# An adaLN block with attention and experts: the setup written out in a fixed order, partly inside the first iterations, with two staging buffers, and the slots blanked from the load queue

## The chip, the cores and the metric

The kernel runs on one core of a Trainium2 chip. The metric is the time of one execution on the device in microseconds. TensorE (PE; its weight loads are PEld) does the matmuls, VectorE is DVE, ScalarE is ACT, GpSimd is POOL, and SyncE (SP) issues most of the DMAs. Every engine works through its own instructions in order; a DMA is issued by an engine's queue and then runs on the core's 16 DMA engines.

## The reference

The input x has 4096 tokens (2 batches of 2048) of width 256. A modulation of six vectors per batch is computed from c, and its two gates are kept away from zero. Then come windowed attention (16 heads of 64, window 128) and a layer of 8 experts, two of which a token uses. The feed-forward layer is cut here to its shape:

```python
mod = (_silu(c) @ wmod).reshape(2, 6, 1, -1)
sa, ca, ga, sb, cb, gb = mod[:, 0], ..., mod[:, 5]
ga = (2 * (ga >= 0) - 1) * jnp.maximum(jnp.abs(ga), 0.25)   # gb likewise
h = layernorm(x) * (1 + ca) + sa
x = x + ga * (window_attention(h @ Wqkv) @ Wout)            # causal, 128 keys
h = layernorm(x) * (1 + cb) + sb
# gate: softmax of h @ gate_w.T + gate_b, top 2; at most 640 slots per expert and choice
# expert: relu(xb @ W1 + b1) @ W2 + b2, weighted by the gate's probability
x = x + gb * experts(h)
```

## The kernel before, in words

**Numbers in two halves.** A product of two fp32 matrices is made of three fp32r matmuls: each operand has an upper half (`hi`, a rounding copy made on ScalarE) and a lower half (`lo`, the rest, a subtraction made on DVE or POOL). `split` makes both from a raw tile, `passes` issues the three matmuls (L232), and `part` (L298) does the split for what comes out of PSUM. A raw piece of weights is 128x1024 fp32, 512 KB.

**Stages.** Up to about 30 us comes the setup (L322 to L463 and the projection at L1159): loading, the modulation, the norm of the first 256 tokens (`norm(0)`, a generator that does one step for each `next`), and the splitting of Wqkv (six pieces) and Wout (two pieces). The raw pieces go into four buffers (two of the pool `stage`, two of the pool `sp`). The order in this part is chosen by a planner that knows costs and dependences. Three small loads, the gate's weights and bias `gw` and `gbias` and the experts' `b1r`, are issued by ScalarE. All the modulation is done here: 16 small matmuls into `mod_cols` (the shift and scale of the first norm, as columns `cols`) and eight into `mod_rows` (the other four vectors), which go through a tile `wide4` and the DRAM tile `rowd` and come back spread over partitions as `rows` and `gbr`.

**Attention.** From the scores of iteration 0 at 29.90 us to about 720 us the kernel is in 64 iterations and three more to drain. A group g is 256 tokens, and each group takes four iterations of two head pairs (four heads). Iteration w runs a software pipeline: it projects q and k for the heads of iteration w+1 (L279), one quarter of v, makes the scores of its own heads (L502), packs the two diagonal blocks with the masks (`pack`, L519 to L527), takes the maximum and starts the exponentials (`exps`, L550); it normalizes the heads of iteration w-1 (L560 on POOL), turns those of w-2 (`turn`, `unpack`, L583) and multiplies them with v (`values`, L607), and applies Wout to those of w-3 (`out_project`). In this part the order is the program's order on all five engines (`manual_schedule`). Work that comes once for each group (the norm of the next group, and `close`, which ends a group: residual, second norm, gate, scatter of the rows to expert slots) is a generator whose steps are put at named places of an iteration by `place(work, w, [...])`. The place "1H" is the point H of iteration w+1; the points come in the order A, B, M, H, C, then the scores, S, V. PSUM tiles for all this come from `bank`, a ring of six.

**Slots.** `xbuf` in DRAM has 10,240 slots of 274 words, which `clear` must blank before the rows of tokens are scattered into them from iteration 12 on (L820). In each of iterations 1 to 4 ScalarE's queue issues four blanking DMAs (L468) of 685 KB from one tile `blank`:

```python
for i in range(2 * w - 2, 2 * w):
    if 0 <= i < E:
        clear(i)          # two DMAs of 640 slots each
```

**Experts.** From about 720 us the slots of each expert are taken in items of up to six tiles of 128; an item has eight steps f, each with a first layer (relu with L939, L940, L941) and, two steps later, a second layer. While the first item of an expert runs, the weights of the next are brought in four pieces at f = 0, 2, 4, 6, each a load (L136) and a split (L127). After the third item the planner orders the instructions again, save those kept in program order, such as these splits.

Of the kernel before, what the change touches and what calls it, by code (L numbers as in the profile page):

```python
# [17 lines left out]
P = 128  # L18
# [10 lines left out]
def adaln_block_kernel(  # L29
# [94 lines left out]
    def split(hi, lo, raw, scale=None, eng=nc.vector, keep=False):  # L124

        if scale is None:
            parts = [nc.scalar.copy(hi, raw), eng.tensor_tensor(lo, raw, hi, ALU.subtract)]  # L127
            for p in parts if keep else ():
                tc.keep_in_program_order(p)
        else:  # L130
            nc.scalar.mul(hi, raw, scale)
            nc.vector.scalar_tensor_tensor(lo, raw, scale, hi, ALU.mult, ALU.subtract)

    def load(src, shape, name, pool=stage):
        raw = pool.tile(shape, FP, tag="raw", name=f"raw_{name}", bufs=2)
        nc.sync.dma_start(out=raw, in_=src)  # L136
        return raw

    def load_split(hi, lo, src, shape, name, scale=None, pool=stage, eng=nc.vector):
        split(hi, lo, load(src, shape, name, pool), scale, eng)  # L140

    class Expert:
# [24 lines left out]
        def use(self, i):  # L167
            wa, wb = self.parts()
            if i < 2:
                s = slice(i * FF // 2, (i + 1) * FF // 2)  # L170
                hi, lo = wa[:, 0, :, s], wa[:, 1, :, s]
            else:
                s = slice((i - 2) * NF // 2, (i - 1) * NF // 2)
                hi, lo = wb[:, 0, s, :], wb[:, 1, s, :]
            split(hi, lo, self.raws.pop(i), keep=self.e > 1)

        def steps(self):

            ahead = 2 if self.e < 2 else 0
            for i in range(ahead):  # L180
                self.get(i)
            if ahead:
                yield
            for i in range(4):
                if not ahead:
                    self.get(i)
                self.use(i)
                if ahead and i + ahead < 4:
                    self.get(i + ahead)
                yield  # L190
# [19 lines left out]
    wk = attn.enter_context(tc.tile_pool(name="work", bufs=2, reuse_waits="tile"))  # L210
    psa = attn.enter_context(tc.tile_pool(name="psa", bufs=2, space=PSUM, reuse_waits="tile"))
# [28 lines left out]
    def norm(g):  # L240
# [13 lines left out]
        for k in range(ND):  # L254
            for t in range(SBT):
                nc.tensor.transpose(
                    tp[:, k * TS + t * P : k * TS + (t + 1) * P], z[:, t, k * P : (k + 1) * P], ident
                )
        hT = wk.tile([P, ND, TS], FP, tag="t2", name=f"hT_{g}")
# [5 lines left out]
        yield  # L265
        hh = wk.tile([P, ND, TS], FR, tag="hh", name=f"hh_{g}")
        hl = wk.tile([P, ND, TS], FR, tag="hl", name=f"hl_{g}")
        nc.scalar.copy(hh, hT)  # L268
        yield
# [50 lines left out]


    first = norm(0)  # L322
    with tc.tile_pool(name="setup", bufs=1) as sp:
        cr = sp.tile([B * ND, P], FP, name="cr")
        nc.sync.dma_start(out=cr, in_=c.rearrange("b (k p) -> (b k) p", p=P))
        xs[0] = load_x(0)
        wm = sp.tile([P, ND, 6 * D], FP, name="wm")
        wmv = wmod.rearrange("(k p) f -> p k f", p=P)
        nc.sync.dma_start(out=wm[:, :, 0 : 2 * D], in_=wmv[:, :, 0 : 2 * D])
        gw = sp.tile([E, D], FP, name="gw")  # L330
        nc.scalar.dma_start(out=gw, in_=gate_w)
        b1r = sp.tile([E * NF, P], FP, name="b1r")
        nc.scalar.dma_start(out=b1r, in_=b1.rearrange("e (k p) -> (e k) p", p=P))
        nc.scalar.dma_start(
            out=gbias, in_=gate_b.rearrange("(a e) -> a e", a=1).to_broadcast([P, E])
        )
        make_identity(nc, ident)

        nc.gpsimd.memset(ones, 1.0)
        nc.gpsimd.affine_select(  # L340
            out=tri, in_=ones, pattern=[[1, P]], compare_op=ALU.is_gt, fill=0.0,
            base=0, channel_multiplier=-1,
        )
        zero = sp.tile([P, P], FP, name="zero")
        nc.gpsimd.memset(zero, 0.0)

        nc.gpsimd.affine_select(
            out=after, in_=zero, pattern=[[-1, P]],
            compare_op=ALU.is_ge, fill=MASKED, base=0, channel_multiplier=1,
        )  # L350

        wf = sp.tile([P, P], FP, name="wf")
        nc.gpsimd.affine_select(
            out=wf, in_=ones, pattern=[[1, P]], compare_op=ALU.is_gt, fill=0.0,
            base=0, channel_multiplier=-1,
        )
        nc.vector.tensor_copy(within, wf)
        irev = sp.tile([P, E], I32, name="irev")
        nc.gpsimd.iota(irev, pattern=[[-P, E]], base=E * P, channel_multiplier=0)
        nc.vector.tensor_copy(rev, irev)  # L360
        nc.gpsimd.iota(tokid, pattern=[[P, NT]], base=0, channel_multiplier=1)
        nc.vector.memset(pref[:, 0, :, :], 0.0)
        nc.vector.memset(eps, EPS)
        nc.vector.memset(mhalf, -0.5)

        next(first)


        sg = sp.tile([B * ND, P], FP, name="sg")
        nc.scalar.activation(sg, cr, AF.Exp, scale=-1.0)  # L370
        nc.vector.tensor_scalar(sg, sg, 1.0, None, ALU.add)
        nc.vector.reciprocal(sg, sg)
        nc.vector.tensor_tensor(sg, sg, cr, ALU.mult)
        tp = bank("tp_c")
        nc.tensor.transpose(tp[:, 0 : B * ND], sg, ident[0 : B * ND, 0 : B * ND])
        scT = sp.tile([P, B, ND], FP, name="scT")
        nc.vector.tensor_copy(scT.rearrange("p b k -> p (b k)"), tp[:, 0 : B * ND])
        mc = bank("mod_cols")
        for m in range(2):
            for d in range(ND):  # L380
                o = (m * ND + d) * B
                for k in range(ND):
                    nc.tensor.matmul(
                        out=mc[:, o : o + B],
                        lhsT=wm[:, k, m * D + d * P : m * D + (d + 1) * P],
                        rhs=scT[:, :, k],
                        start=(k == 0),
                        stop=(k == ND - 1),
                    )
        colf = cols.rearrange("p m d b -> p (m d b)")  # L390
        nc.vector.tensor_copy(colf[:, 0 : ND * B], mc[:, 0 : ND * B])
        nc.vector.tensor_scalar(
            colf[:, ND * B : 2 * ND * B], mc[:, ND * B : 2 * ND * B], 1.0, None, ALU.add
        )

        for _ in first:
            pass

        for i in range(2):
            for j in range(3):  # L400
                f = slice(j * HD + i * HD // 2, j * HD + (i + 1) * HD // 2)
                load_split(
                    wq[:, 0, :, f], wq[:, 1, :, f], wqkv[:, f].rearrange("(k p) f -> p k f", p=P),
                    [P, ND, HD // 2], f"wq{i}_{j}", QSCALE if j == 0 else None,
                    pool=sp if (3 * i + j) % 2 else stage,
# [680 lines left out]
    def iteration(w):  # L1086
        g, p2 = divmod(w, NP // 2)
        if p2 == NP // 2 - 1 and g + 2 < NG:
            xs[g + 2] = load_x(g + 2)
# [220 lines left out]
```

## Time and profile before

| | us |
|---|---|
| median of 3 runs | 1154.32 |
| lowest, highest | 1153.67, 1157.11 |
| the profiled execution: its time | 1156.12 |
| the profiled execution: its span in the trace | 1154.4 |
| busy in the span: PE, DVE, ACT, POOL | 1078.9, 876.5, 677.6, 592.8 |
| mean granted TensorE clock | 0.975 of full speed |
| scores of iterations 0 to 6 start at | 29.90, 40.93, 52.27, 68.04, 78.75, 92.96, 102.73 |

Times in the trace count from the start of the span. In a row of the timeline the first number is the start, the second the length, then come engine, line, operation, and the tile written and those read; what stands in brackets is the idle time of the engine before the instruction and what ended it. ACTq and SPq are the queues from which ScalarE and SyncE issue DMAs; these issues do not count as busy time. The granted clock is the share of full speed that TensorE was given. A line of waits gives the idle time in total, how often, and the longest.

### The profile page before, as it was taken

Reading aid. Unit: us, or ns where it says so; the run is one execution under the profiler, and the core shown is the slowest. Engines: PE = TensorE matmul, PEld = TensorE weight load, DVE = VectorE, ACT = ScalarE, POOL = GpSimd, SP = SyncE. Lnnn points to the kernel's source line nnn. Section 1 sums busy time; section 2 is a strip of 40 time slices with the busy share of each in tenths; the row PEclk is TensorE's granted clock in tenths of the full one; section 3 lists DMA queues with packets and bytes.
Section 4 is the critical chain, followed back from the end, with each engine's and each line's share of the span. In section 5 each row is a group of like instructions: output and inputs, shape, how many; then the busy total and the mean of one; then the engine's idle time right before and its main releaser. Section 6 shows DMA issues by size and latency. Waiting matters only on the chain. (4 is left out here: it accounts for less than half of the span.)

```text
span 1154.4 us, 25197 instructions
## 1 busy us (share of the span) xinstructions
PE 1078.9 (93%) x9246; PEld 991.9 (86%) x9246; DVE 876.5 (76%) x2168; ACT 677.6 (59%) x2097; POOL 592.8 (51%) x769
## 2 busy tenths in 40 slices
PE   6799999999999989999999998688899999999995
PEld 4579999998998979989999997577799999999995
DVE  6656687887888778887887877677677777878774
ACT  4467776776776657776776766433444444344441
POOL 4235465665665556665665655534242615443524
PEclk9889999999999999999999999879999999999998
DMA  6790000010010010000000012243352524343413
GB/s 229 188 226 21 2 31 28 21 34 25 21 39 20 21 34 30 30 26 21 27 28 26 21 54 65 72 108 90 83 134 81 84 86 89 85 88 68 85 43 36
DMA packets 59587, 72.09 MB, mean 62 GB/s; under 512 B 4823, under 2 KB 51168, under 8 KB 59452
## 3 DMA queue, kind: packets, MB, share of 16 engines
q1 hardware_dynamic: 37004, 44.27, 12.6%
q0 software_dynamic: 11712, 14.79, 7.4%
q10 hardware_dynamic: 10736, 11.27, 4.3%
q8 instruction: 80, 1.31, 0.5%
q14 instruction: 55, 0.45, 0.1%
HBM read 40.11 MB, written 32.27 MB: 63 GB/s over the span
## 5 line engine op out<-in xcount | busy, mean ns | idle before, releaser
L939 ACT ACTIVATE hm<-ph,b1T 128x256 fp32r<-128x256 f32 (+2 forms) x184 | 99.2, 539 | 214.3 <-PE ph L232 175.8
L232 PE MATMUL pq<-hh,wq 128*128 128x256 f32 x1024 | 214.8, 294 | 4.6 <-ACT hh L268 4.0
L550 ACT ACTIVATE pm<-pm,mx 128x128 f32<-128x128 f32 x512 | 204.0, 402 | 17.9 <-DVE mx L536 15.2
L232 PE MATMUL ph<-xT,we 128*128 128x256 f32 (+2 forms) x1104 | 198.1, 320 | 9.7 <-PEq L1244 3.7
L232 PE MATMUL y<-we,hm 128*128 128x256 f32 x1440 | 200.9, 284 | 6.2 <-DVE hm L941 6.1
L232 PEld LDWEIGHTS y<-we,hm 128*128 128x128 f32 x1440 | 185.9, 190 | 9.5 <-DVE hm L941 8.4
L584 POOL TENSOR_SCALAR_AFFINE_SELECT pT<-pT 128x512 f32<-128x512 f32 (+1 forms) x128 | 80.1, 626 | 212.5 <-ACT pT L583 212.4
L232 PEld LDWEIGHTS ph<-xT,we 128*128 128x128 f32 x1104 | 167.7, 191 | 15.0 <-issue 5.1
L232 PEld LDWEIGHTS pq<-hh,wq 128*128 128x128 f32 x1024 | 168.4, 192 | 7.2 <-ACT hh L268 4.4
L940 DVE TENSOR_SCALAR r<-ph,b1T 128x256 f32<-128x256 f32 (+2 forms) x184 | 101.8, 562 | 64.1 <-ACT hm L939 55.9
L560 POOL TENSOR_TENSOR pm<-pm,rd 128x512 f32<-128x512 f32 x128 | 133.4, 1042 | 26.4 <-DVE rd L558 26.4
L232 PE MATMUL pq<-hl,wq 128*128 128x256 f32 x512 | 144.9, 283 | 0.0
L526 ACT COPY pm<-sc 128x256 f32<-128x256 f32 (+1 forms) x256 | 80.7, 363 | 109.2 <-PE sc L502 72.0
L1004 POOL TENSOR_TENSOR ys<-ys,gw 128x256 f32<-128x256 f32 x56 | 47.1, 926 | 170.4 <-DVE ys L994 167.7
L607 PE MATMUL av<-pT,v 128*64 128x128 f32 (+1 forms) x1472 | 125.8, 320 | 4.5 <-POOL pT L588 1.5
L607 PEld LDWEIGHTS av<-pT,v 128*64 128x64 f32 x1472 | 90.3, 139 | 33.4 <-POOL pT L588 4.0
L1005 POOL DMA_INDIRECT out_dram<-ys,tok x60 | 97.6, 1627 | 31.5 <-issue 11.5
L527 DVE COPY_PREDICATED pm<-within,sc 128x256 f32<-128x256 int32 (+1 forms) x256 | 96.0, 422 | 22.6 <-ACT pm L526 21.8
L502 PE MATMUL sc<-kr,qh 64*128 64x256 f32 (+1 forms) x1024 | 106.6, 297 | 6.3 <-DVE ql L300 2.9
L550 ACT ACTIVATION_READ_ACCUMULATOR pm<-pm,mx 128x1 f32 x512 | 99.5, 194 | 0.0
L941 DVE TENSOR_TENSOR hm<-r,hm 128x256 fp32r<-128x256 f32 (+2 forms) x144 | 95.2, 661 | 5.0
L232 PE MATMUL po<-wo,ah 128*128 128x256 f32 x512 | 98.3, 285 | 0.0
(166 smaller groups left out, 2262.9 us busy)
## 6 DMA issues: line engine op xcount, KB each, us to landing
raw_w<-in_L_ffn_W_dram SPq DMA_DIRECT2D x32, 512.0 KB, 3.9
xbuf<-blank ACTq DMA_DIRECT2D x16, 685.0 KB, 9.4
xt<-xbuf SPq DMA_DIRECT2D x7, 822.0 KB, 4.8
xt<-xbuf SPq DMA_DIRECT2D x8, 548.0 KB, 5.0
x<-in_L_attn_x_dram SPq DMA_DIRECT2D x16, 256.0 KB, 2.8
out_dram<-x SPq DMA_DIRECT2D x16, 256.0 KB, 2.3
raw_wq<-in_L_attn_Wqkv_dram SPq DMA_DIRECT2D x6, 512.0 KB, 7.4
wm<-in_L_wmod_dram SPq DMA_DIRECT2D x1, 1024.0 KB, 12.1
```

What stands on the lines that cost most here:

```text
L232: nc.tensor.matmul(out=out_, lhsT=a, rhs=b, start=start and n == 0 and i == 0, stop=stop and n == last and i == 2, **kw,)
L502: nc.tensor.matmul(out=sc[h][:, t, lo:], lhsT=q[r, t * P : (t + 1) * P], rhs=kr[r, (0, 1, 0)[i], hp, blk, :], start=(i == 0), stop=(i == 2),)
L526: nc.scalar.copy(pm[:, h, ts, :], blocks[:, own, :])
L527: nc.vector.copy_predicated(pm[:, h, ts, :], within.rearrange("p (a k) -> p a k", a=1).to_broadcast([P, n, P]), blocks[:, before, :],)
L550: nc.scalar.activation(pm[:, h, t, :], pm[:, h, t, :], AF.Exp, bias=mx[:, h, t : t + 1], accum_out=den[:, h, t : t + 1],)
L560: nc.gpsimd.tensor_tensor(pmv, pmv, rd.rearrange("p h (t a) -> p (h t) a", a=1).to_broadcast([P, 2 * SBT, P]), ALU.mult,)
L584: nc.gpsimd.affine_select(out=pT[:, :, t0:, 0, :], in_=own[:, :, t0:, :], pattern=[[0, 2], [0, n], [-1, P]], compare_op=ALU.is_gt, fill=0. ...
L607: nc.tensor.matmul(out=av[h * DH : (h + 1) * DH, q0 : q0 + hi - lo], lhsT=v[:, f0 + h * DH : f0 + (h + 1) * DH], rhs=pT[:, h, lo:hi], star ...
L939: nc.scalar.activation(hh[:, s], phv, AF.Relu, bias=bias)
L940: nc.vector.tensor_scalar(r[:, s], phv, bias, 0.0, ALU.add, ALU.max)
L941: nc.vector.tensor_tensor(hl, r[:, 0:W], hh, ALU.subtract)
L1005: add = nc.gpsimd.indirect_dma_start(out=of, out_offset=bass.IndirectOffsetOnAxis(ap=tok[:, 0:1], axis=0), in_=y, in_offset=None, bounds_c ...
```

## The change

1. The whole setup is now in the program's fixed order on all engines. In it the modulation is done in three parts: the shift and scale of the first norm as two wide matmuls (`modulation(0)`), a copy to SBUF by ScalarE, and four small transposes to `cols`; the other two parts come later. For group 0 ScalarE makes `hh` straight from PSUM beside DVE's `hT`.
2. The raw pieces of Wqkv and Wout go through the two buffers of `stage` alone. `high(n)` is the upper half of piece n on ScalarE, `low(n)` the lower half (on DVE for Wqkv, on POOL for Wout) followed by the load of piece n+2 into the buffer that it frees. Pieces 0 to 2 are done in the setup; 3 to 7, the other two parts of the modulation (`load_mod`, `modulation`), the turning of the gate weights and of b1, and the loads of `rows` and `gbr` are the generator `second_half`, placed in iterations 0 to 3. The three small loads go from ScalarE's queue to SyncE's, the load of x for group 1 goes forward, that for group 2 to the end of iteration 2.
3. `clear` issues one DMA of 640 slots from SyncE's queue; two are issued in each of iterations 1 to 8. The pool of the setup is closed and the pool `early` opened before iteration 9.
4. Among the experts all weights are loaded two pieces ahead: five pieces at f = 0, 2, 3, 4, 6, the first of which only loads, and the loads of slots stand ahead of the piece.

The diff, cut:

```diff
-    def load(src, shape, name, pool=stage):
-        raw = pool.tile(shape, FP, tag="raw", name=f"raw_{name}", bufs=2)
+    def load(src, shape, name):
+        raw = stage.tile(shape, FP, tag="raw", name=f"raw_{name}")
         nc.sync.dma_start(out=raw, in_=src)
...
+    def upper(hi, raw, scale=None):
+        return nc.scalar.copy(hi, raw) if scale is None else nc.scalar.mul(hi, raw, scale)
+    def lower(hi, lo, raw, scale=None, eng=nc.vector):
+        if scale is None:
+            return eng.tensor_tensor(lo, raw, hi, ALU.subtract)
+        return eng.scalar_tensor_tensor(lo, raw, scale, hi, ALU.mult, ALU.subtract)
...
         def steps(self):
-            ahead = 2 if self.e < 2 else 0
-            for i in range(ahead):
+            for i in range(2):
                 self.get(i)
-            if ahead:
-                yield
+            yield
             for i in range(4):
-                if not ahead:
-                    self.get(i)
                 self.use(i)
-                if ahead and i + ahead < 4:
-                    self.get(i + ahead)
+                if i < 2:
+                    self.get(i + 2)
                 yield
...
+    order = tc.manual_schedule(engines=everything)
+    order.__enter__()
     first = norm(0)
...
+    def load_mod(m):
+        wms[m] = sp.tile([P, ND, 2 * D], FP, tag="wm", name=f"wm_{m}")
+        nc.sync.dma_start(out=wms[m], in_=wmod...[:, :, 2 * m * D : (2 * m + 2) * D])
...
+    def high(n):
+        next(parts_[n])
+    def low(n):
+        next(parts_[n], None)
+        if n + 2 < len(parts_):
+            next(parts_[n + 2])
+    for n in range(2):
+        next(parts_[n])
+    xs[1] = load_x(1)
...
+    def modulation(m):
+        mr = bank(f"mod_{m}")
+        for k in range(ND):
+            nc.tensor.matmul(out=mr[0:B, :], lhsT=scT[:, :, k], rhs=wms[m][:, k, :], ...)
+        return mr
+    mr = modulation(0)
...
+    high(0)
+    next(first)
+    low(0)
+    next(first)
+    high(1)
+    part(*project_qk(0, 0, 0))
+    low(1)
+    high(2)
+    part(*project_qk(0, 0, 1))
+    low(2)
...
+    def second_half():
+        for n in range(3, 8):
+            if n == 5:
+                load_mod(1)
+            high(n)
+            yield
+            low(n)
+            if n < 6:
+                yield
+        xs[2] = load_x(2)
+        yield
...
         for g in range(2):
+            mr = modulation(g + 1)
+            if g == 0:
+                load_mod(2)
...
+            nc.sync.dma_start(out=rowd[:, 2 * g : 2 * g + 2, :], in_=wide)
+            yield
         load_rows(0)
...
     def clear(i):
-        for r0 in range(i * BUF, (i + 1) * BUF, CAP):
-            nc.scalar.dma_start(
+        nc.sync.dma_start(
...
-    NORM = ["0B", "1A", "1H", "2A", "2B"]
+    NORM = ["0B", "1A", "1H", "1H", "2A", "2B"]
+    SECOND = "0B 0M 0M 0S 1B 1S 1V 2B 2V 3A 3A 3V 3V".split()
...
-            if 0 <= i < E:
+            if 0 <= i < E * KC:
                 clear(i)
...
+    place(second_half(), 0, SECOND)
     for w in range(NW + 3):
+        if w == E * KC // 2 + 1:
+            start.close()
+            early = attn.enter_context(tc.tile_pool(name="early", bufs=1, ...))
         iteration(w)
...
+    PIECES = (0, 2, 3, 4, 6)
-        more = {f: [do(piece, e + 1)] for f in (0, 2, 4, 6)}
-        more[0].append(do(load_slots, q + 1, q2 - q - 2))
+        more = {f: [do(piece, e + 1)] for f in PIECES}
+        more[0].insert(0, do(load_slots, q + 1, q2 - q - 2))
```

## The prediction

> **What bounds the kernel now.** I read the page first, then the windows cut at the first score matmul of each attention iteration (starts from the timeline), then ScalarE's timeline and the waits inside the worst windows. The page gives the whole:
>
> ```profile
> PE 1078.9 (93%) x9246; PEld 991.9 (86%) x9246; DVE 876.5 (76%) x2168; ACT 677.6 (59%) x2097; POOL 592.8 (51%) x769
> PE   6799999999999989999999998688899999999995
> DMA  6790000010010010000000012243352524343413
> ```
>
> TensorE is the bound nearly everywhere; apart from the change of stage near 720 to 790 us it has room only in the first four slices of 29 us, which are also the slices in which DMA is full. In the windows below, columns are length, busy us (instructions) of PE, PEld, DVE, ACT, POOL, then granted clock and DMA share:
>
> ```profile
> 0.00:15.60 15.60, 4.76 (x21) 4.30 (x21) 6.44 (x21) 6.30 (x7) 6.09 (x17) 1.00 0.80 279
> 15.60:29.90 14.30, 13.98 (x65) 8.23 (x66) 12.88 (x15) 6.54 (x9) 7.66 (x5) 1.00 0.48 157
> 29.90:40.93 11.03, 7.70 (x58) 6.22 (x59) 8.51 (x23) 2.99 (x13) 2.01 (x3) 1.00 0.43 139
> 40.93:52.27 11.34, 9.58 (x63) 8.35 (x62) 5.98 (x16) 5.70 (x23) 1.04 (x1) 0.70 1.01 232
> 52.27:68.04 15.77, 13.20 (x91) 10.97 (x90) 7.12 (x18) 9.88 (x37) 5.57 (x9) 0.78 1.04 224
> 68.04:78.75 10.71, 10.21 (x91) 8.93 (x91) 5.15 (x16) 5.05 (x20) 2.69 (x4) 1.00 1.00 228
> 78.75:92.96 14.21, 12.71 (x95) 10.46 (x95) 8.34 (x21) 11.56 (x40) 9.21 (x14) 0.88 0.61 129
> 92.96:102.73 9.77, 9.77 (x91) 8.79 (x91) 6.97 (x15) 8.05 (x28) 3.74 (x6) 1.00 0.00 1
> ```
>
> From 92.96 on an iteration is all PE: 10.2, 10.7, 11.5 and 10.2 us follow, and that cycle holds for most of the stage. So whatever the change does to the moment at which the scores of iteration 6 start (102.73) goes into the end one for one; what it does elsewhere must show at PE. Three losses stand before it: 29.9 us of setup, iterations of 15.8 and 14.2 us, and half clock (0.70, 0.78, 0.88). ScalarE's timeline shows where two of them come from:
>
> ```profile
> 50.44 1.30 ACTq L468 DMA_DIRECT2D xbuf<-blank  x1
> 50.56 0.19 ACT L550 ACTIVATION_READ_ACCUMULATOR pm<-pm,mx 128x1 f32 x1
> 51.77 1.50 ACTq L468 DMA_DIRECT2D xbuf<-blank  x1
> 53.31 0.59 ACT L583 COPY pT<-tp 128x512 f32<-128x512 f32 x1 [2.55 <-PE pv L232]
> ...
> 74.62 2.03 ACTq L468 DMA_DIRECT2D xbuf<-blank  x1
> ...
> 76.69 2.08 ACTq L468 DMA_DIRECT2D xbuf<-blank  x2
> 78.87 0.59 ACT L583 COPY pT<-tp 128x512 f32<-128x512 f32 x1 [2.86 <-PE pv L232]
> ```
>
> The releaser named (PE pv) had long been done: the copy starts when ScalarE has finished issuing blanking DMAs. There are 16 such issues of 0.52 to 2.03 us, 16.5 us in all, four in each of iterations 1 to 4; behind them ScalarE idled 2.45 (until 41.30), 2.55, 1.94 (until 65.89) and 2.86 us. PSUM banks that ScalarE has not emptied then hold PE, which shows as waits of the score matmuls (L502) for L299, L300 and L583.
>
> **The change, part by part.** The profiled execution took 1156.12 us, its span 1154.4 plus 1.7 around it; the median of the three runs is 1154.32, so I take the gain from the trace and set it against the median.
>
> *Setup.* Before, the first projection matmul ran at 15.63 but the rest of it only at 22.32: PE was in between with eight mod_rows matmuls (0.85 us apart until about 21 us, 0.43 after) and DVE with two lower halves delayed by POOL (one took 3.09 where another took 1.23). New order: ScalarE no longer issues three small loads ahead of its table load (0.82 to 2.71, table load at 2.74), so the exponential comes at about 3.0; DVE's sg chain and the statistics end at 6.2; two modulation matmuls of 0.85 to 8.0; copy 0.6; z transposes 1.1 and four small transposes 0.8 to 9.9; cols, hT (0.99) and hh to 11.4; low(0) 1.22 and hl 0.68 to 13.3. The first weights landed at 9.96 with 2 MB queued, here with 1 MB, so they are no later. Projection q ends at 16, its ql at 17.2; only then low(1), 18.4; projection k at 20.5; iteration 0's q, k, v at 1.43 each: scores of iteration 0 at about 25.0 instead of 29.9. **Gain 4.9.** DVE takes six lower halves of Wqkv where it took three and one of Wout (+2.4 us); POOL drops from four to two (3.33 each at worst), in iteration 2 beside 2.7 to 5.6 us of own work. Those are covered by POOL's idle time; without it the next turn would wait 3 us.
>
> *Two staging buffers.* This adds a wait. A load takes 4.0 us (raw_wo row), then high 1.05, low 1.22 before its buffer is free. Piece 4 (k, second half) is loaded after low(2), at 23.1, lands at 27.1; high(4) sits on ScalarE (0M) ahead of the mask copies of iteration 0, done 28.2; then the two packs as in the trace (first copy 33.84 to last predicated copy 37.63: 3.8) and low(4) behind them on DVE (0S): 33.2. Queued behind high(4): pack copies and exponentials. Waiting for low(4): PE, with k of pair 2, from about 28. Hence 5 us of idle PE and then k, v and the transposes of norm(1). A rule speaks here. The row first: the half clock of window 40.93:52.27 came after waits no longer than 2.1 us:
>
> ```profile
> PE tp_h L256 <- DVE z L248: 2.7, 2, 2.1
> ```
>
> The Trainium skill (TensorE: Matmul & The Clock Gate, HAM oscillation) puts the limit at idle gaps above about 3.4 us. If the load is quicker and the hole is 2.5 us, the rule gives no half clock and PE work of 3.4 us; the row gives half clock and 6.2. I take the row: scores of iteration 1 at 33.2 + 6.0 = 39.2 against 40.93. **Iteration 0 gives back 3.2.** Bounds: 1 (rule) to 6 (load at the 7.4 of the raw_wq row).
>
> *Blanks on SyncE's queue.* ScalarE loses 16.5 us of issuing. A rule speaks against this as well: DMA: Bandwidth & Descriptors (Issuing engines are not separate DMA queues) says all queues run on the same 16 engines, so another issuer saves only the issue time, "usually small relative to the DMA itself". With SyncE's usual 0.37 us that is 6 us on an engine 5.7 of 11.3 us busy: nothing at PE. The rows say 1.3 to 2.0 us for the later issues and 9.8 us of ScalarE idle; I take the rows, but only for what PE lost. Iteration 1: 11.34 to 10.0 (pace of its PE work with part of it at half clock). Iteration 2: 15.77 to 13.0 (steady 10.6, plus the gate and b1 transposes and two warm modulation matmuls, 1.3 in all, plus 1 of PSUM waits). Iteration 4: 14.21 to 11.5, its steady length; iteration 5: 9.77 to 10.2.
>
> *Modulation in iteration 3 and what is queued on SyncE.* wm_1 follows two blanks in iteration 1 and is read in 3A, an iteration later: covered. wm_2 is loaded after the matmuls that read wm_1 (3A), behind blanks that SyncE, waiting for nothing, has issued already: 16 blanks held DMA full for about 50 us, 3.1 each. Wout's second half goes out at 43.7, then four blanks and x2, 14 us of transfer, until 58; wm_2 lands at about 61, and PE reaches 3V near 60. I book 1 us of wait, 0.9 of matmuls: 10.71 to 12.6. Ends: nothing, or 10. x2 goes out before iteration 3 and is wanted in 4B; gw, b1r, gbias follow x1 and are wanted in iteration 3; rows and gbr from iteration 6: all covered by whole iterations. Blanks end near iteration 9, the first scatter is in iteration 12.
>
> *Experts.* Five pieces at f = 0, 2, 3, 4, 6 instead of four; the first only loads. An extra 1.22 falls on DVE at f = 3, where the expert-head window 864 to 868 shows 2.54 of 4.00 us; loads were already issued two ahead (761.48, 764.59). Zero; if DVE were full there, 1.22 for each of six heads.
>
> **Sum**: 4.9 - 3.2 + 1.3 + 2.8 - 1.9 + 2.7 - 0.4 = 6.2 us, so 1148.1.
>
> **The rivals.** *The hole does not open* (chance 0.26): the pieces come as fast as the first four did (ScalarE started on them at 9.96, 11.30, 12.67 and 14.02, as they landed), PE waits 2 us and stays warm; another 5 to 6: 1142.5. Against it: each load has to wait for its buffer.
> *Staging as slow as the table's 7.4 us* (0.16): high(4) at 32, scores of iteration 1 at 43.5, the gain down to about 2: 1152.5, no change by the 0.3% (3.5 us) that a measurement of this kernel can tell. For it: the row's median; against: those loads were queued four deep.
> *The blanks starve wm_2* (0.12, slower): PE stands at 3V until the load behind four blanks lands. If it lands 10 us after PE gets there, PE pays 9 more than booked and 3.4 us of half clock: 12.4 - 6.2 = +6, 1160. It decides from a wait of about 7 us on; it needs blanks at more than 3.1 us each, or PE earlier at 3V than I have it. For it: the DMA share of 1.00 wherever blanks run now; against: two blanks for each iteration instead of four.
> *The moved issues never reached PE* would leave only setup minus the hole: 1.7, inside the second rival.
>
> **How the numbers follow.** Forecast 1148.1 with 0.46 (1145 to 1150.8); the rivals 0.26, 0.16, 0.12. Faster 0.72, same 0.16, slower 0.12. The range 1140 to 1155 leaves out the far end of the first rival and most of the last.
>
> **What would show it.** Right: score starts near 25, 39, 49, 62, 75, 86 and 96 instead of 29.9 to 102.73; no ACTq issues; ScalarE's idle behind L583 gone; a PE wait on wq L132/L127 in iteration 0 with half clock after it; DMA share near 0.6 until 120 us; everything from there shifted by the same 6 us. Wrong: a PE wait for wm in iteration 3 above 3 us, a DMA wait of ScalarE at a high(n) after iteration 1, or expert heads longer than before.

## The result, and the profile after

Measured side by side on one chip, the changed kernel takes 1148.32 us (median of 4 runs, 1147.94 to 1148.94) and the kernel before 1155.12 us (4 runs, 1153.67 to 1157.11). The ratio is 0.994 (95% interval 0.9923 to 0.9958), so 6.8 us are gained. The profiled execution took 1148.45 us with a span of 1146.7 and a mean granted clock of 0.977. From the page, the engines in total and the rows of TensorE and DMA over 40 slices:

```profile
PE 1077.6 (94%) x9238; PEld 991.4 (86%) x9238; DVE 874.0 (76%) x2170; ACT 678.0 (59%) x2099; POOL 587.0 (51%) x767
PE   6799999999999999999999997788899999999995
DMA  4866200000000010010010022233353434343413
```

The work is the same; DMA is now spread over five slices at the start. The windows, cut again at the first score matmuls of iterations 0 to 6 (columns: length, busy us and instructions of PE, PEld, DVE, ACT, POOL, then granted clock, DMA share, GB/s):

```profile
0.00:13.00 13.00, 5.44 (x14) 1.83 (x14) 5.49 (x20) 3.81 (x6) 3.42 (x17) 1.00 0.47 165
13.00:27.43 14.43, 11.72 (x54) 10.61 (x54) 6.97 (x13) 5.52 (x8) 0.42 (x2) 1.00 0.36 106
27.43:38.96 11.53, 8.28 (x60) 7.09 (x60) 8.37 (x19) 8.08 (x26) 2.63 (x3) 0.85 0.47 137
38.96:46.64 7.68, 7.12 (x63) 6.16 (x62) 5.54 (x15) 4.13 (x16) 0.00 (x0) 1.00 1.00 195
46.64:63.90 17.26, 14.47 (x99) 10.86 (x99) 9.95 (x27) 12.32 (x42) 13.12 (x14) 0.90 1.03 238
63.90:75.42 11.52, 11.52 (x96) 8.98 (x96) 8.39 (x25) 7.19 (x27) 3.85 (x7) 1.00 0.07 15
75.42:85.63 10.21, 10.21 (x95) 9.20 (x94) 5.74 (x14) 7.63 (x27) 5.42 (x8) 1.00 1.09 262
85.63:95.40 9.77, 9.77 (x91) 8.78 (x90) 6.98 (x15) 8.15 (x28) 3.88 (x6) 1.00 1.00 211
```

The scores of iteration 6 start at 95.40 instead of 102.73, which is 7.3 us earlier, and the last scores of the stage at 719.90 instead of 726.81, 6.9 earlier. So all of it is decided before 96 us, as forecast, but not where it was forecast: the setup ends only 2.5 us earlier (27.43), iteration 1 is down to 7.7 us, and iteration 2 is longer than before, 17.3 us, and the only one with POOL at 13. What PE waited for between 27.4 and 95.4 us (idle time in total, times, longest):

```profile
PE pq L230 <- DVE wq L135: 3.2, 1, 3.2
PE av L676 <- ACT v L326: 1.4, 1, 1.4
PE sc L571 <- DVE ql L308: 1.2, 1, 1.2
```

The first is the hole of iteration 0. The other two lie in iteration 2, and behind each of the two places comes half clock (a granted clock of 0.50): 35.1 to 38.5 and 52.2 to 55.6 us, 6.8 us in all, where the profile of before had 17.1 us of it. After 56 us PE waits for nothing.

One warning on the size of such readings. The same attention program, in the run of the kernel before with only the experts' part changed (E3 below), starts iteration 6 at 99.77, not at 102.73. Iteration 0 starts at 25.64 to 27.60 in the six profiles that share this setup (27.43 here is among the latest) and at 28.86 to 30.42 in the six that have the old one. And the time from the last scores to the end of the span varies between 425.7 and 429.7 us over the fourteen profiles of this case, without order. So a single trace places a loss, and the comparisons of many runs say what it is worth.

### The profile page after: what moved, and what is told of

Same layout as the page of the kernel before. It is cut to its first block, busy times and chain, and to the rows that moved or that the text cites. A ratio compares the mean times of both kernels' runs of the same rounds, so it can differ in the third digit from the quotient of the medians.

```text
span 1146.7 us, 25186 instructions
## 1 busy us (share of the span) xinstructions
PE 1077.6 (94%) x9238; PEld 991.4 (86%) x9238; DVE 874.0 (76%) x2170; ACT 678.0 (59%) x2099; POOL 587.0 (51%) x767
## 3 DMA queue, kind: packets, MB, share of 16 engines
q1 hardware_dynamic: 48016, 55.54, 17.1%
## 5 line engine op out<-in xcount | busy, mean ns | idle before, releaser
L230 PE MATMUL pq<-hh,wq 128*128 128x256 f32 x1024 | 217.9, 297 | 7.8 <-DVE wq L135 5.4
L230 PEld LDWEIGHTS pq<-hh,wq 128*128 128x128 f32 x1024 | 170.8, 194 | 10.3 <-DVE wq L135 5.8
L676 PEld LDWEIGHTS av<-pT,v 128*64 128x64 f32 x1472 | 89.7, 138 | 33.2 <-issue 3.5
L596 DVE COPY_PREDICATED pm<-within,sc 128x256 f32<-128x256 int32 (+1 forms) x256 | 96.1, 422 | 24.9 <-ACT pm L595 23.8
L571 PE MATMUL sc<-kr,qh 64*128 64x256 f32 (+1 forms) x1024 | 102.5, 294 | 1.4 <-DVE ql L308 1.2
L230 PEld LDWEIGHTS pq<-hl,wq 128*128 128x128 f32 x512 | 99.6, 195 | 0.9 <-DVE hl L278 0.9
```

What stands on the lines that cost most here:

```text
L230: nc.tensor.matmul(out=out_, lhsT=a, rhs=b, start=start and n == 0 and i == 0, stop=stop and n == last and i == 2, **kw,)
L571: nc.tensor.matmul(out=sc[h][:, t, lo:], lhsT=q[r, t * P : (t + 1) * P], rhs=kr[r, (0, 1, 0)[i], hp, blk, :], start=(i == 0), stop=(i == 2),)
L596: nc.vector.copy_predicated(pm[:, h, ts, :], within.rearrange("p (a k) -> p a k", a=1).to_broadcast([P, n, P]), blocks[:, before, :],)
L676: nc.tensor.matmul(out=av[h * DH : (h + 1) * DH, q0 : q0 + hi - lo], lhsT=v[:, f0 + h * DH : f0 + (h + 1) * DH], rhs=pT[:, h, lo:hi], star ...
```

## The experiments

The blanks and the experts' part are told apart by making one alone or undoing one; the setup's order and the two buffers are only seen together. With each experiment stand the expectations written ahead of it.

**E1: the changed kernel with the blanks as before** (four per iteration in iterations 1 to 4, from ScalarE's queue).

```diff
-        nc.sync.dma_start(out=xbuf[i * CAP : (i + 1) * CAP, :]..., in_=blank...)
+        for r0 in range(i * BUF, (i + 1) * BUF, CAP):
+            nc.scalar.dma_start(out=xbuf[r0 : r0 + CAP, :]..., in_=blank...)
...
-            if 0 <= i < E * KC:
+            if 0 <= i < E:
```

> The changed kernel with the blanks as before: four for each of iterations 1 to 4, issued by ScalarE. Theory Q (ScalarE's issuing was what PE waited for in iterations 2 and 4, and the setup alone brings some 2.5 us): ScalarE idles about 2.5 us again ahead of the pT copies, iterations 2 and 4 are long again, and 4 to 5 us of the 6.8 are lost: about 1152.5 to 1153.5. Theory S (the earlier and less idle start carries it; the queue saves issue time on an engine with time to spare): within 1.5 us of the changed kernel, 1148 to 1150.

Measured: 1155.5 us, ratio to before 1.0008 (0.9999 to 1.0017; before 1154.83). Without the moved blanks nothing is left of the gain. Iteration 2 takes 22.89 us. The waits of ScalarE and of PE in it:

```profile
ACT wo L131 <- DMA raw_wo<-in_L_attn_Wout_dram: 3.9, 1, 3.9
```

```profile
PE av L676 <- ACT v L326: 4.7, 1, 4.7
```

The load of a piece of Wout left SyncE at 46.16, when two of ScalarE's four blanks were out and the third was being issued; ScalarE stands before the upper half of this piece until 56.31, the copy of v stands behind it on ScalarE, and PE stands before the values. The new setup thus loses to these blanks twice: by ScalarE's issues, as before, and by a load that comes late.

**E2: the kernel before with the blanks of the change alone** (SyncE, two per iteration, iterations 1 to 8).

```diff
-        for r0 in range(i * BUF, (i + 1) * BUF, CAP):
-            nc.scalar.dma_start(
-                out=xbuf[r0 : r0 + CAP, :]...
+        nc.sync.dma_start(
+            out=xbuf[i * CAP : (i + 1) * CAP, :]...
...
-            if 0 <= i < E:
+            if 0 <= i < E * KC:
```

> The kernel before with only the blanks changed: two for each of iterations 1 to 8, issued by SyncE. Theory Q: 4 to 5 us faster than before (about 1150.5), with iterations 2 and 4 shortened by 3 to 4 us each. Theory S: 1154 to 1155.5, no difference. A third possibility: slower, if x or the residual's store behind the blanks on SyncE's queue comes late; then waits for x appear in iterations 4 to 8.

Measured: 1144.76 us, 0.9914 (0.99 to 0.9929): 10 us less than before, with one of the four parts, and 3 us more than the whole change gains. "Two per iteration" holds for the program only: SyncE waits for nothing here and issues the first twelve blanks between 23.1 and 48.1 us. The windows of iterations 1 and 2, and then those of the same kernel in its second profile (E12):

```profile
39.74:49.49 9.75, 9.75 (x64) 9.00 (x64) 5.89 (x16) 5.97 (x24) 3.08 (x4) 0.67 1.11 257
49.49:60.10 10.61, 10.20 (x92) 8.93 (x92) 6.40 (x17) 7.68 (x29) 4.22 (x8) 1.00 1.12 226
```

```profile
39.47:46.56 7.09, 7.09 (x63) 6.36 (x63) 5.10 (x15) 3.31 (x14) 1.04 (x1) 1.00 1.12 260
46.56:60.00 13.44, 11.12 (x91) 9.36 (x90) 7.33 (x19) 10.51 (x40) 6.25 (x10) 1.00 1.10 238
```

The two iterations have to be taken together: one profile has 6.8 us of half clock in iteration 1 and 0.4 us of waits in iteration 2, the other no half clock and 2.3 us of waits in iteration 2, and they are done at 60.1 and 60.0. The copy of v that PE waits for in iteration 2 comes at 50.71 and 50.60, so ScalarE's chain of work sets this end, and the half clock of the first profile cost nothing. Together the iterations take 20.4 and 20.5 us, where they took 27.1 before and take 24.9 in the changed kernel. Iteration 4 takes 10.22 instead of 14.21. At iteration 6 this kernel is 5.3 us ahead of the changed one (90.10 and 95.40): in these traces that is what the new setup and its pieces cost when the blanks are out of the way. Something else is in the 10 us too: with the blanks on SyncE the planner orders DVE's work in the setup another way (a lower half of q comes ahead of the second gate's signs), and iteration 0 takes 9.3 us instead of 11.0.

**E3: the kernel before with the experts' part alone.**

```diff
-            ahead = 2 if self.e < 2 else 0
...
+            for i in range(2):
+                self.get(i)
+            yield
...
+    PIECES = (0, 2, 3, 4, 6)
-        more = {f: [do(piece, e + 1)] for f in (0, 2, 4, 6)}
+        more = {f: [do(piece, e + 1)] for f in PIECES}
```

> The kernel before with only the experts' loading changed (two pieces ahead, five places). Both theories: the same as before within 1 us (1154 to 1156), since the loads were two ahead already and DVE has room at f = 3. Rival: the experts carry part of the 6.8 us, then 1152 or less; or DVE becomes late in the heads, then up to 7 us more.

Measured: 1154.63 us, 0.9996 (0.999 to 1.0003). The experts' part is worth nothing that this comparison can see.

**E4: the changed kernel with the lower half of piece 4 placed earlier** in iteration 0, ahead of the packs on DVE.

```diff
-    SECOND = "0B 0M 0M 0S 1B 1S 1V 2B 2V 3A 3A 3V 3V".split()
+    SECOND = "0B 0M 0M 0C 1B 1S 1V 2B 2V 3A 3A 3V 3V".split()
```

> The changed kernel with one step moved: the lower half of piece 4 stands ahead of the packs of iteration 0 on DVE (place 0C) instead of behind them (0S). Theory D (the 3.2 us wait of PE for wq in iteration 0 is DVE's order, not a load that comes late): the wait falls under 1 us, there is no half clock after it, scores of iteration 1 near 36.5 instead of 39, and the packs come 1.5 us later; the end 0 to 2 us earlier, since iteration 2 then waits for ScalarE as before. Theory L (the load of piece 4 is late): PE waits as long as before, now with the packs late as well: 1 to 2 us slower.

This asks whose fault the hole is. The prediction put it under the two buffers and began its chain with the load of piece 4. In the changed kernel that load, issued at 24.41 and 3.8 us under way, landed as ScalarE came free, and the upper half began at 28.28; but the lower half stood behind the packs on DVE until 32.92. From the timeline of the changed kernel:

```profile
28.28 1.05 ACT L131 CAST wq<-raw_wq 128x1024 fp32r<-128x1024 f32 x1
28.52 0.28 DVE L588 TENSOR_TENSOR pm<-sc,after 128x128 f32<-128x128 f32 x1
...
32.92 1.22 DVE L135 TENSOR_TENSOR wq<-raw_wq,wq 128x1024 fp32r<-128x1024 f32 x1
34.19 0.50 PE L230 MATMUL pq<-hh,wq 128*128 128x256 f32 x2 [3.25 <-DVE wq L135]
```

Measured: 1149.11 us, 0.9949 (0.9935 to 0.9962; the changed kernel has 0.994 and, taken again in E11, 0.9934). The order of DVE was the cause of this wait, and yet taking it away gains nothing, since DVE's packs and norm are now late by what the lower half takes. The waits of PE in this kernel:

```profile
PE tp_h L254 <- DVE z L246: 3.6, 2, 3.0
PE pq L230 <- DVE wq L135: 0.5, 1, 0.5
```

The wait for the weights shrank from 3.2 to 0.5 us, and the transposes of the norm of group 1 wait 3.6 us in its place; half clock follows here too (35.7 to 42.6). In iteration 0 DVE has two kinds of work to give to PE, and either order keeps PE waiting.

**E5 and E6: what it was in the blanks that cost 10 us.** E2 changed two things, the issuing engine and the number at a time. E5 changes the number alone (two per iteration, iterations 1 to 8, still ScalarE), E6 in the program the engine alone (four per iteration, iterations 1 to 4, SyncE). Both are edits to the kernel before:

```diff
# E5
-        for r0 in range(i * BUF, (i + 1) * BUF, CAP):
-            nc.scalar.dma_start(
+        nc.scalar.dma_start(
+            out=xbuf[i * CAP : (i + 1) * CAP, :]...
...
-            if 0 <= i < E:
+            if 0 <= i < E * KC:
# E6
-            nc.scalar.dma_start(
+            nc.sync.dma_start(
```

> The kernel before with two blanks for each of iterations 1 to 8 instead of four in 1 to 4, still issued by ScalarE. Theory N (what costs is the third and fourth issue of a burst, 1.3 to 2.0 us each against 0.52 and 0.67 for the first two): ScalarE's idle behind the issues goes, and this is within 2 us of the same blanks on SyncE's queue (about 1145 to 1147). Theory E (ScalarE is too full to issue blanks at all): half the gain at most, 1149 to 1152.

> The kernel before with the blanks of before in number and place (four in iterations 1 to 4) issued by SyncE. Theory N and theory E both: SyncE stands in its bursts and nobody waits, 1144 to 1146. If instead it is the density of the blanks in the DMA engines that costs (a load behind four blanks comes late), 1149 or more, with a wait of ScalarE or DVE for a load.

Measured: E5 1146.53 us, 0.9903 (0.9887 to 0.992); E6 1144.38 us, 0.9884 (0.9868 to 0.9901); before 1157.36. Either change alone brings 10 us or more. E6 is not quite the engine alone: SyncE runs ahead, so its blanks start at 23.15, 14 us before ScalarE's would, and the planner's other order in the setup is in it as in E2 (iteration 0 takes 9.4 us; in E5 11.1, as before). E5 has neither, and its 10.8 us are the blanks' own. In E5 ScalarE still issues, but each pair costs 0.52 and 0.67 us and the copies come straight behind:

```profile
46.75 0.52 ACTq L467 DMA_DIRECT2D xbuf<-blank  x1
47.30 0.67 ACTq L467 DMA_DIRECT2D xbuf<-blank  x1
48.43 0.57 ACT L583 COPY pT<-tp 128x512 f32<-128x512 f32 x1
```

In E6 it is SyncE that stands there, and nobody waits for SyncE. The timeline of its queue (a row of x8 runs eight issues together):

```profile
23.15 14.04 SPq L468 DMA_DIRECT2D xbuf<-blank  x8
...
42.44 21.53 SPq L468 DMA_DIRECT2D xbuf<-blank  x7
```

Fifteen issues take 35.6 us there, 2.4 us each, against 0.5 to 0.7 in E5's pairs. So the cost was neither ScalarE as an issuer nor the four blanks in the DMA engines: it was the later issues of a run, which take 1.3 to 2.0 us each on ScalarE, with the copies that empty PSUM waiting in order behind them.

**E7: the changed kernel with Wout's second half later.** In the changed kernel ScalarE works without a pause from 43.66 to 51.65 us, and two upper halves of Wout, 1.03 and 1.05 us, stand in this chain; the copy of v is at its end:

```profile
45.21 1.03 ACT L131 CAST wo<-raw_wo 128x1024 fp32r<-128x1024 f32 x1
46.15 0.57 ACT L652 COPY pT<-tp 128x512 f32<-128x512 f32 x1
...
49.65 1.05 ACT L131 CAST wo<-raw_wo 128x1024 fp32r<-128x1024 f32 x1
51.06 0.59 ACT L326 COPY v<-pv 128x512 f32<-128x512 f32 x1
51.80 2.49 PE L676 MATMUL av<-pT,v 128*64 128x256 f32 x16 [1.43 <-ACT v L326]
```

The edit moves both upper halves to later points of iteration 2 and the last lower half, with what follows it, into iteration 3:

```diff
-    SECOND = "0B 0M 0M 0S 1B 1S 1V 2B 2V 3A 3A 3V 3V".split()
+    SECOND = "0B 0M 0M 0S 1B 1S 2M 2V 3A 3A 3A 3V 3V".split()
```

> The changed kernel with the two pieces of Wout done later (upper halves at 2M and 2V instead of 1V and 2B, lower halves at 2V and 3A). Theory A (iteration 2 of 17.3 us is long because 2.1 us of upper halves stand in ScalarE's unbroken chain from 43.7 to 51.6, which PE waits for): iteration 2 falls to about 14, its half clock goes, and the end is some 3 us earlier, 1145. Rival theory P (POOL's two lower halves of 2.35 and the modulation matmuls make it long): no change, 1147.5 to 1149.

Measured: 1147.66 us, 0.9917 (0.9899 to 0.9935). Its window of iteration 2:

```profile
45.12:60.20 15.08, 12.94 (x100) 9.73 (x99) 10.14 (x27) 12.08 (x40) 9.78 (x10) 1.00 1.05 232
```

17.26 us become 15.08 and the half clock is gone. That is 2.2 us by the windows; by the ratio, whose interval overlaps that of the changed kernel, it can't be told from nothing. In the trace ScalarE's chain is thus one cause of the long iteration 2, but iterations 1 and 2 together still take 22.8 us, against the 20.4 of E2.

**E8: the changed kernel with four raw buffers.** Two more come from the memory of a tile that is not yet in use; loads run four pieces ahead, each lower half in the setup stands on DVE ahead of the projection's own, piece 3 is done in the setup, and all others, Wout too, by the end of iteration 1.

```diff
-    def load(src, shape, name):
-        raw = stage.tile(shape, FP, tag="raw", name=f"raw_{name}")
+    def load(src, shape, name, pool=stage, tag="raw"):
+        raw = pool.tile(shape, FP, tag=tag, name=f"raw_{name}")
...
-        if n + 2 < len(parts_):
-            next(parts_[n + 2])
+        if n + 4 < len(parts_):
+            next(parts_[n + 4])
...
     high(1)
-    part(*project_qk(0, 0, 0))
     low(1)
+    part(*project_qk(0, 0, 0))
     high(2)
-    part(*project_qk(0, 0, 1))
     low(2)
+    high(3)
+    low(3)
+    part(*project_qk(0, 0, 1))
...
-    SECOND = "0B 0M 0M 0S 1B 1S 1V 2B 2V 3A 3A 3V 3V".split()
+    SECOND = "0B 0M 0S 0V 1A 1M 1H 1V 2M 2V 3V 3V".split()
```

> The changed kernel with four staging buffers (two borrowed from tiles that are first used in iteration 2), four pieces loaded at the start, each lower half of the setup ahead of the projection's own, and the last pieces done by iteration 1. Theory B (two buffers and the steps they push into iterations 1 to 3 are what the new setup loses): scores of iteration 0 at about 24.5, no wait of PE for wq in iteration 0, iteration 2 near 13 us, scores of iteration 6 at 87 to 90 instead of 95.4: 1141 to 1143. Rival theory C (ScalarE and DVE are full in iterations 0 and 1 whatever the order): iteration 0 and 1 become longer by what iteration 2 gains, 1147 or more.

Measured: 1143.35 us, 0.9874 (0.9857 to 0.989). The scores of iteration 0 start at 23.63 and those of iteration 6 at 89.96, 5.4 us ahead of the changed kernel. There is no wait for weights any more, but the transposes of the norm wait 2.8 us, half clock comes at 33.2 to 40.0 and 46.9 to 50.3, and iteration 2 has 14.65 us. With four buffers, and the order that they allow, the new setup thus brings more; the edit changes both, so which of them it is isn't shown, and E2 and E12 are a warning not to book the half clock that remains as a loss.

**E9: the changed kernel with its blanks, two per iteration, from ScalarE.**

```diff
-        nc.sync.dma_start(
+        nc.scalar.dma_start(
             out=xbuf[i * CAP : (i + 1) * CAP, :]...
```

> The changed kernel with its blanks (two for each of iterations 1 to 8) issued by ScalarE. If the burst of four is what costs (as the blanks of before, cut to two, showed), this stays within 2 us of the changed kernel, a ratio of 0.993 to 0.996 to before. If it is ScalarE as the issuer, it lies near the changed kernel with the blanks of before, a ratio of 0.998 or more.

Measured: 1151.36 us, 0.9959 (0.9945 to 0.9973; before 1156.01). By the medians it is some 3 us slower than the changed kernel, where 2 at most were expected after E5; the ratio is at the end of the expected range. The issues were cheap again, 0.52 and 0.67 us; the cost came by another way. From ScalarE's and then SyncE's timeline of E9, and SyncE's of the changed kernel:

```profile
43.52 0.52 ACTq L539 DMA_DIRECT2D xbuf<-blank  x1
44.07 0.67 ACTq L539 DMA_DIRECT2D xbuf<-blank  x1
...
52.80 1.05 ACT L131 CAST wo<-raw_wo 128x1024 fp32r<-128x1024 f32 x1 [3.05 <-DMA raw_wo<-in_L_attn_Wout_dram]
```

```profile
45.27 0.37 SPq L126 DMA_DIRECT2D raw_wo<-in_L_attn_Wout_dram  x1
```

```profile
45.28 0.37 SPq L126 DMA_DIRECT2D raw_wo<-in_L_attn_Wout_dram  x1
45.70 1.22 SPq L539 DMA_DIRECT2D xbuf<-blank  x2
```

The load leaves SyncE at the same moment in both. On one queue it stands ahead of the two blanks; with two queues both blanks are already out, and ScalarE waits 3.05 us for its data. Iteration 2 takes 20.94 us. What SyncE's queue gives the changed kernel is thus also an order: its loads go before its blanks.

**E10: E8 with the pieces earlier still.** Piece 4 is done in the setup, piece 5 ahead of the packs, the two gate parts of the modulation in iterations 1 and 2, Wout late in iteration 2.

```diff
+    high(4)
+    low(4)
...
-    SECOND = "0B 0M 0M 0S 1B 1S 1V 2B 2V 3A 3A 3V 3V".split()
+    SECOND = "0B 0M 1B 2M 2V 2V 3A 3V".split()
```

> The kernel with four staging buffers, and besides: piece 4 done in the setup, piece 5 ahead of the packs of iteration 0, the first gate's modulation in iteration 1 where PE waits, the second in iteration 2, Wout late as in the run that moved it. Theory B: scores of iteration 0 near 24, no wait of PE for z, iterations 0 to 2 at 9, 9 and 12.5 us, scores of iteration 6 at 85 to 87: a ratio of 0.983 to 0.985, the fastest of all. Theory C (ScalarE and DVE are full there): no faster than the four buffers alone, 0.987 or more.

Measured: 1141.79 us, 0.9879 (0.9864 to 0.9894). Expected was 0.983 to 0.985. It has the lowest median of all and 22.45 as the start of the scores, but its ratio can't be told from those of E6 and E8. The windows of its iterations 1 and 2:

```profile
33.06:43.83 10.77, 10.09 (x64) 9.11 (x63) 7.07 (x22) 5.51 (x20) 2.46 (x4) 0.68 0.81 218
43.83:57.25 13.42, 12.61 (x98) 9.67 (x97) 9.23 (x27) 11.02 (x38) 8.12 (x9) 1.00 0.13 43
```

Iteration 1 has its half clock (34.0 to 40.8) although from 24 us on PE waited no longer than 1.1 us at a time before it. Any of E6, E8 and E10 is about 1.2% faster than the kernel before; E6 differs from it by one word.

**E11 and E12: the changed kernel and E2 again, on one chip.** No edit is new.

> The changed kernel itself, once more, on the same chip as the run beside it. A ratio near 0.994 to before, as the first time.

> The kernel before with the changed kernel's blanks alone, once more, beside the changed kernel. If the new setup with its pieces in iterations 0 to 3 costs time once the blanks are out of the way, this is 3 to 4 us faster than the changed kernel, as between the separate runs. If that was a difference of chips, the two are within 1 us.

Measured: 1148.31 us, 0.9934 (0.992 to 0.9948) and 1145.49 us, 0.9909 (0.9895 to 0.9923); before 1156.02. With the blanks moved in both, the rest of the change makes it 2.8 us slower. The traces repeat: iteration 6 starts at 95.54 (95.40) and 90.00 (90.10). Their gap of 5.5 us is larger than the 2.8 of the medians; part of it lies behind the last scores, where these two profiles take 426.1 and 427.7 us, and both profiles of the changed kernel have a late start (27.43 and 27.60). Since E3 found nothing in the experts and the stretch behind the last scores varies by 4 us anyway, where the rest goes is left open.

Where the changed kernel loses can be read from its profile beside E12's. It starts iteration 0 2.6 us earlier; iteration 0 takes 2.1 us more, iteration 1 0.6, iteration 2 3.8 and iteration 3 1.5. In iteration 2 the values come only 0.5 us later (51.80 and 51.33); behind them stand 2.3 us of PE work that the setup had before (the turning of the gate's weights and b1, and a part of the modulation) and 3.4 us at half clock. The other part of the modulation is in iteration 3:

```profile
55.78 1.88 PE L455 MATMUL mod<-wm,scT 128*2 128x512 f32 x4
66.92 1.88 PE L455 MATMUL mod<-wm,scT 128*2 128x512 f32 x4
```

The setup of the changed kernel leaves PE idle for 10.3 of 27.4 us; iteration 2 leaves it 2.8 us and iteration 3 nothing. No run takes it out alone.

## Why the prediction was right, and where its sum was not

The forecast, 1148.1 us, is 0.2 from the median, and its sum of 6.2 stands against 6.8 measured. The place was right (all before iteration 6) and so was the sign of most steps. But the total was right by luck, by two errors that cancel: the blanks, booked at 6.8, are worth 10 us, and the rest of the change, booked at a loss of 0.6, costs some 3 (2.8 between E12 and E11; with the old blanks, E1, 0.9, within its uncertainty of nothing). At iteration 6 the trace has, term by term, +2.5 for the setup, then -0.5, +3.7, -1.5, -0.8, +4.0 and 0 for iterations 0 to 5, 7.3 in all; booked were +4.9, -3.2, +1.3, +2.8, -1.9, +2.7 and -0.4.

- **Setup, booked +4.9, measured +2.5 by the start of the scores** (3.5 between the means of six profiles each). Two terms failed. The first is a count: two modulation matmuls of 0.85 us were booked, and the trace has four, since each of the program's two shows as two:

```profile
5.79 3.57 PE L455 MATMUL mod<-wm,scT 128*2 128x512 f32 x4 [0.94 <-DMA wm<-in_L_wmod_dram]
```

  Part of that was hidden; low(1) was done 0.9 us later than booked (19.3 for 18.4). What the prediction foresaw for the queue on DVE (ql, only then low(1)) came as a wait of 2.1 us. The second term is PE's pace: the projections ran at about half pace until 24.9 us, and k of the setup and the q, k and v of iteration 0, booked at 6.6 us, took 8.1. Two rows of the changed kernel show the same pair of matmuls, slow and then fast:

```profile
24.01 0.63 PE L230 MATMUL pq<-hh,wq 128*128 128x256 f32 x2
...
25.12 0.41 PE L230 MATMUL pq<-hh,wq 128*128 128x256 f32 x2
```

  In the kernel before, PE was at full pace from about 21 us on (the prediction's own rows had it, 0.85 us apart, then 0.43), and eight extra modulation matmuls had kept it busy until then. That taking them out of the setup also took away what warmed PE for the projections is argued from this. It agrees with this that in E8, where lower halves stand earlier and PE's wait of 2.1 us is gone, the fast pace begins at about 19.6 and the scores at 23.63.
- **Hole of iteration 0, booked 5 us of wait and a loss of 3.2; measured 3.25 us of wait, and iteration 0 longer by 0.5 (11.53 against 11.03; 14.2 was forecast).** The working's chain was nearly right: upper half done at 28.2 and lower half at 33.2, where the trace has 29.3 and 34.1. The wait was shorter because PE came to it at 30.94, not at 28, and the half clock behind it began only 0.9 us after its end. The heading was wrong: no load was late, and it is the packs before low(4) on DVE, named in the working, that set the wait (E4).
- **The rule on half clock.** Against the rule that PE should have no idle gaps above about 3.4 us (the Trainium skill, TensorE: Matmul & The Clock Gate, HAM oscillation), the row was taken, and the row held: half clock came behind a wait of 3.25 us, behind 1.4 in iteration 2 and behind waits of at most 1.1 us in E10. In the 6.8 us ahead of the three PE had been busy for 3.55, 4.01 and 5.06 us. It is not the busy share of such a stretch alone either: in E12 PE was busy for 4.58 of the 6.8 us from 45.1 to 51.9 and PE had full clock there and after; and behind the same two waits for the norm in iteration 0 (2.0 us, longest 1.3) E2 has 6.8 us of half clock and E12 none. What decides stays open.
- **Iteration 1, booked +1.3, measured +3.7** (11.34 to 7.7). It ran at full clock, where 10.0 had assumed half clock in part.
- **Iteration 2, booked +2.8, measured -1.5** (15.77 to 17.26). This is the largest miss; with iteration 1 it is +2.2 where 4.1 was booked. The step took the ScalarE issues out and put the small transposes and two modulation matmuls in, 1.3 us in all; they took 2.3, since there are four again. It left out what else the change moves there: two upper halves of Wout in ScalarE's chain, the lower halves on POOL at 2.35 us each (booked as covered), and half clock behind the waits that follow. With the blanks alone iterations 1 and 2 take 20.4 us together (E2, E12), so in the trace the pieces cost 4.5; E7 shows 2.2 of them to be the place of Wout and the half clock that goes with it.
- **Iteration 3, booked -1.9, measured -0.8** (12.6 and 11.52). The wait of 1 us for wm_2 did not come: the load was issued at 57.69 and its matmuls ran at 66.92 without a wait. They took 1.88 us where 0.9 was booked.
- **Iterations 4 and 5, booked +2.7 and -0.4, measured +4.0 and 0** (11.5 and 10.2; 10.21 and 9.77). With no half clock left they fell to their steady pace at once: 1.7 us more than booked.
- **Blanks against the rule** that another issuer only saves issue time, "usually small relative to the DMA itself" (the Trainium skill, DMA: Bandwidth & Descriptors, Issuing engines are not separate DMA queues). Right is that the DMA engines are the same: four at a time cost nothing from SyncE (E6). That only issue time is at stake fits E5 and E6 but not E9, where a load on the other queue came late. Small it is not: the later issues of a run took 1.3 to 2.0 us, up to two thirds of the 3.1 us of a blank's transfer, in an engine whose copies PE needs. Taking the row was right, but it was booked at what iterations 1, 2 and 4 seemed to lose, 6.8 us, and against that stood steps that belong to the setup. On its own it is 10.
- **Experts, booked at zero:** 0.9996 (E3).

The rivals: the hole opened, though by DVE and not by loads. Staging as slow as 7.4 us was not seen. The blanks did not starve wm_2; but its mechanism, a load behind blanks and PE behind the load, is real and cost PE 4.7 us in E1 and ScalarE 3.05 in E9, both times for Wout. That the issues never reached PE is refuted by E5. One reading of the page was loose: PE is at 6 and 7 tenths in the first two slices and at 9 from the third on, and DMA is at 6, 7 and 9 tenths in the first three and at 0 in the fourth.

Not tried: taking the modulation alone out of iterations 2 and 3 of the changed kernel, and E6's blanks together with the buffers of E8. How much of iteration 2 is POOL's lower halves also stays open, and so does what the setup's new order brings without the two buffers.

## What to carry to other kernels

An engine that issues DMAs pays for a run of them in its own order: read the length of the third and fourth issue, not of the first, then see who stands behind them, and issue them in smaller numbers or from a queue that nobody waits for. Such a queue runs ahead, so the transfers then also start earlier (E6: 14 us). Loads with a reader and transfers without one are safer on one queue, loads first; on two queues the bulk got ahead here (E9). Work moved out of a setup must find room where it goes. Half clock in a trace is a loss only if PE's end is what the next step waits for (E2 and E12). And a total that comes out right says little about its terms: make the parts one by one, since here one part alone beats the whole.

## What the runs showed of the hardware that was not expected

- The price of issuing the same 685 KB transfer: 0.52 to 0.67 us for the first two of a run on ScalarE and 1.3 to 1.5 for later ones (in the fourth run it was the second that took 2.03), and 2.4 on average over fifteen on SyncE (E6). On SyncE a pair took 1.22 to 2.45 us in the changed kernel, so the price is not ScalarE's alone. That a full queue is the reason is argued.
- The clock column reads 1.00 for the whole of the setup in this profile, although pairs of matmuls take 0.63 us until 24.9 and 0.41 after. In four of the six profiles of this setup it does show half clock for a part of the time (0.50 from 12 to 21 us in E4). For a cold start the duration of a known matmul is the better witness.
- The length of the cold part changes from run to run: in the six profiles of the same setup the pairs are fast from about 22.0 us (E4, E9) to 25.1 (E11), and the scores start between 25.64 and 27.60.
- Half clock came mostly in stretches of 3.4 or about 6.8 us (35.1 to 38.5 and 52.2 to 55.6 in the changed kernel, 33.2 to 40.0 and 46.9 to 50.3 in E8, 34.0 to 40.8 in E10), behind waits as short as 1.1 us. The same program can have it in one profile and not in another (E2 and E12), and start iteration 3 at the same time (60.1 and 60.0).
